# A mixture of eight experts with a residual: seven tiles of 128 pairs taken ahead of the routing tables, not eight, and the work of the routing in another order

## The chip, the cores and the metric

The kernel runs on one core of one Trainium2 chip. The metric is the device time of one execution in microseconds; before the change the median of three runs is 450.62 us (449.47 to 450.69). Engines are called as in the profile: PE is TensorE's matmul side and PEld its loading of the stationary operand, DVE is VectorE, ACT is ScalarE, POOL is GpSimd, SP is the queue that starts most transfers.

## The reference

4096 tokens (64 x 64) of 256 features, 8 experts, the best 2 per token, so 8192 (token, expert) pairs. Cut to what matters:

```python
var = jnp.mean(x * x, axis=-1, keepdims=True)
xn = rms_w * (x * jax.lax.rsqrt(var + EPS))
gate = xn @ wg_W + wg_b + (genre_embed @ gg_W + gg_b)
gate_w = jax.nn.softmax(gate, axis=-1)
topk_w, topk_i = jax.lax.top_k(gate_w, 2)
cw = sum over the two of one_hot(topk_i, 8) * topk_w
h1 = relu(einsum('bsh,ehm->bsem', x, W1) + b1)      # 256 -> 512, each expert
h2 = relu(einsum('bsem,emn->bsen', h1, W2) + b2)    # 512 -> 512
out_e = einsum('bsen,enh->bseh', h2, W3) + b3       # 512 -> 256
return x + einsum('bseh,bse->bsh', out_e, cw)
```

The reference computes all eight experts for every token; the weights `cw` of six of them are zero, and the kernel computes only the two that count. With these inputs the experts get 830, 1246, 851, 1202, 1139, 912, 767 and 1245 pairs.

## The kernel before, in words

**Two parts of the tokens.** A partition holds 32 tokens (`NI`), of which the first 8 (`NA`) are part A and the other 24 part B. Part A (1024 tokens) is routed first, in `first_part`: sums of squares (`squares`), transposes (`turn`), gate products, the two best experts (`choose`), running counts of each expert (`inc`), ranks of the tokens inside their expert (`ranks`, two small matmuls that need `inc`), and totals. From part A alone the kernel builds eight **single tiles** of 128 pairs, one for each expert (`E` = 8): every expert has at least 175 pairs in part A. Their indices are `idxA`.

**The single tiles** are the head of the program. `head_step(u, more)` runs tile u: layer 1, then the transposes of tile u+1, layer 3 of tile u-1, and layer 2 of tile u. A product here is plain: 8 products of 128 columns in layer 1 (L1046), 16 in layer 2 (L1056), 4 of 256 columns in layer 3 (L1325). The profile counts each fp32 product as two instructions.

**The routing of part B** is worked out meanwhile, mainly on DVE, by the generator `rest()`: norms and choice of part B, its ranks and totals, the layout of the remaining pairs into units, a position for each pair, and then four chunks of 16 columns of one-hot tables. A chunk is three DVE instructions: `ohl` (which row of a tile, L777), `ohh` (which tile, L779) and `ohv` (`ohh` times the token's number, L782); 16 fp16 products on PE (L616) add each chunk up to the table of indices `idxR`. `head_step` calls `more(ns)` to let the generator run for about so many ns (the numbers after `yield`), and `table(n)` to issue the table's products on PE. Then `gather_unit` fetches rows on POOL's queue with `idxR`. All engines run in the order in which the code issues.

**The units.** What the single tiles leave is laid out by expert in units of up to 4 tiles (512 pairs), in steps of 32 pairs. Units of two or more tiles run a Strassen scheme: 7 products of blocks in place of 8 (`Fast` for layers 1 and 2, L1155; `Wide` for layer 3, L1257). An expert's pairs are split into units of 16 steps (512 pairs), at most one pair of tiles (8 steps) and a last unit of 9 to 16 steps. The list of units is one of 46 arms of a switch: 32 of them are the rows of `SHAPES` (number of 16-step units, number of experts with an 8-step unit, steps of the last units), chosen on the chip by the counts. Here the first row is taken: five units of 16, then 16, 9, and then pairs of (15, 8), (14, 8), (12, 8), (11, 8), (11, 8), (10, 8). Expert 7 has 1245 - 128 = 1117 pairs left, 35 steps: 16 + 8 + 11.

**The seam.** The last head step waits for the table, gathers units E and E+1, and starts their weights' transfers on SP's queue; `fill` copies x to the output in four parts (the residual), and `give` adds each finished tile to the output by an indirect transfer on POOL's queue, in chains that wait for the unit before. Unit E (`step_fast` with u == E) transposes its four tiles on PE; the later units go through a DRAM buffer (`stow`, `shuffle`) and are transposed on DVE.

## Time and profile before

| what | us |
|---|---|
| median of the runs | 450.62 (449.47 to 450.69) |
| the profiled execution | 450.4 |
| its span, first to last instruction | 448.7 |
| PE busy | 440.1 (98%) |
| DVE busy | 358.3 (80%) |
| ACT busy | 259.2 (58%) |
| POOL busy | 274.5 (61%) |
| first single tile starts (L1046) | 23.17 |
| first unit starts (L937) | 87.03 |

The time of the profiled execution is 1.7 us above its span. The span has three stages: up to 23.17 us the gates of part A and the first gathers; to 87.03 us the eight single tiles, beside which DVE works out the routing of part B; and then 19 units. In rows of the timeline the columns are the start, the duration (for groups, from first start to last end), the engine, the line, the operation and its operands, and in brackets how long the engine sat idle before and what ended that. PE's ends are modelled, so that rows of PE overlap a little: the price of a group is the distance from its start to the start of the next.

### The profile page before, as it was taken

How to read it: one execution, taken by the hardware profiler on the slowest of the kernel's cores; microseconds unless marked ns; L12 is line 12 of the kernel's file. 1: busy time of each engine (PE TensorE's matmuls, PEld its weight loads, DVE VectorE, ACT ScalarE, POOL GpSimd, SP SyncE). 2: the span in 40 equal slices, each digit the busy share in tenths (PEclk: the TensorE clock that was granted, in tenths of full speed). 3: DMA queues.
4: the chain of work that ended last, by engine and by line, in shares of the span. 5: the costliest groups of instructions: out<-in, count | busy, mean ns of one | idle time of the engine just before them, and what ended most of it. 6: DMA issues, size and time to landing. Idle time of an engine off the chain costs nothing.

```text
span 448.7 us, 9511 instructions
## 1 busy us (share of the span) xinstructions
PE 440.1 (98%) x3096; PEld 414.2 (92%) x3096; DVE 358.3 (80%) x985; ACT 259.2 (58%) x624; POOL 274.5 (61%) x235
## 2 busy tenths in 40 slices
PE   8999999999999999999999999999999999999994
PEld 7689999988989999999999899999999999999984
DVE  5898995677798888888899977977978879779851
ACT  5855543456465555646475655755755765566642
POOL 4347433857888875837475764874775766666342
PEclk9999999999999999999999999999999999999999
DMA  8799999784657657545564663474464565555123
GB/s 291 271 345 374 383 362 384 276 260 84 185 163 138 164 94 199 93 118 103 145 117 99 117 139 92 68 166 106 66 166 107 120 135 117 124 108 105 18 24 39
DMA packets 71600, 72.51 MB, mean 162 GB/s; under 512 B 34736, under 2 KB 60819, under 8 KB 71157
## 3 DMA queue, kind: packets, MB, share of 16 engines
q1 hardware_dynamic: 48976, 43.29, 29.9%
q0 software_dynamic: 14960, 17.50, 23.6%
q10 hardware_dynamic: 7604, 11.02, 8.1%
q8 instruction: 26, 0.43, 0.4%
q14 instruction: 34, 0.27, 0.2%
HBM read 56.34 MB, written 20.12 MB: 170 GB/s over the span
## 4 chain that ended last, share of the span: by engine, by line
PE 93%; DVE 3%; issue 1%; POOLq 1%; POOL 1%; ACT 0%; DVEq 0%
PE pb L1155 55%; PE pb L1257 18%; PE pb L1056 6%; PE pb L1325 4%; PE pb L1046 3%; PE pb L254 1%; PE pb L616 1%; PE pb L482 1%; POOL out_dram L1357 1%; PE pb L937 1%; PE pb L285 1%; DVE xT L925 0%; PE pb L291 0%; DVE big L1132 0%; POOLq L1680 0%
## 5 line engine op out<-in xcount | busy, mean ns | idle before, releaser
L1357 POOL DMA_INDIRECT out_dram<-ys,idxR x57 | 98.4, 1727 | 82.0 <-DVE ys L1356 64.9
L1155 PE MATMUL pb<-hid,big 128*128 128x256 f32 (+7 forms) x456 | 83.2, 326 | 0.0
L1176 ACT ACTIVATE hid<-hid,bb 128x256 f32<-128x256 f32 (+12 forms) x154 | 72.9, 524 | 11.2 <-DVE hid L1170 10.6
L870 POOL DMA_INDIRECT cg<-cwdR,idxR x59 | 63.9, 1083 | 18.0 <-issue 18.0
L1155 PEld LDWEIGHTS pb<-hid,big 128*128 128x128 f32 x456 | 70.4, 191 | 4.2 <-ACT hid L1176 0.8
L1164 ACT COPY big<-pb 128x512 f32<-128x512 f32 (+7 forms) x57 | 27.1, 476 | 65.8 <-PE pb L1155 51.0
L1155 PE MATMUL pb<-mixB,big 128*128 128x256 f32 (+7 forms) x304 | 55.5, 325 | 0.1
L1155 PE MATMUL pb<-hotA,big 128*128 128x256 f32 (+7 forms) x304 | 55.3, 325 | 0.0
L1155 PEld LDWEIGHTS pb<-mixB,big 128*128 128x128 f32 x304 | 47.9, 191 | 3.1 <-ACT bc L1034 0.5
L1155 PEld LDWEIGHTS pb<-hotA,big 128*128 128x128 f32 x304 | 46.6, 191 | 2.1
L1155 PE MATMUL pb<-mixX,iotx 128*128 128x256 f32 (+7 forms) x228 | 46.5, 327 | 0.0
L870 POOL DMA_INDIRECT big<-in_x_dram,idxR x32 | 35.5, 1110 | 9.8 <-issue 8.2
L1155 PEld LDWEIGHTS pb<-mixX,iotx 128*128 128x128 f32 x228 | 36.6, 191 | 2.9 <-issue 0.8
L870 POOL DMA_INDIRECT xgE<-in_x_dram,idxR x27 | 30.5, 1128 | 13.0 <-issue 12.1
L1164 ACT COPY q1s<-pb 128x512 f32<-128x512 f32 (+7 forms) x57 | 26.9, 472 | 18.6 <-PE pb L1155 17.0
L1278 DVE TENSOR_TENSOR ys<-pb,big 128x128 f32<-128x128 f32 (+1 forms) x54 | 18.7, 346 | 23.4 <-PE pb L1257 16.7
L1056 PEld LDWEIGHTS pb<-hid,w2a 128*128 128x128 f32 x256 | 29.8, 192 | 1.1 <-ACT hid L1049 0.8
L1155 PE MATMUL pb<-xT,w1r 128*128 128x256 f32 (+7 forms) x152 | 30.8, 325 | 0.0
L1056 PE MATMUL pb<-hid,w2a 128*128 128x128 f32 x256 | 30.5, 276 | 0.0
L1266 ACT COPY big<-pb 128x128 f32<-128x128 f32 (+1 forms) x54 | 16.6, 307 | 23.3 <-PE pb L1257 23.3
L925 DVE STREAM_TRANSPOSE xT<-gTs 128x256 f32<-128x256 f32 x55 | 29.4, 644 | 0.6 <-DMA gTs<-scr 0.6
L1034 ACT ACTIVATE bc<-b_sb,cw 128x256 f32 x59 | 26.1, 498 | 6.4 <-DVE cw L1017 5.5
(349 smaller groups left out, 926.4 us busy)
## 6 DMA issues: line engine op xcount, KB each, us to landing
w2a<-in_L_cond_W_dram SPq DMA_DIRECT2D x8, 1024.0 KB, 12.9
w1r<-in_L_cond_W_dram SPq DMA_DIRECT2D x11, 512.0 KB, 15.0
w3r<-in_L_cond_W_dram ACTq DMA_DIRECT2D x11, 512.0 KB, 4.3
w3r<-in_L_cond_W_dram SPq DMA_DIRECT2D x10, 512.0 KB, 11.5
w1r<-in_L_cond_W_dram ACTq DMA_DIRECT2D x10, 512.0 KB, 3.6
gTs<-scr SPq DMA_DIRECT2D x7, 512.0 KB, 4.0
out_dram<-in_x_dram SPq DMA_DIRECT2D x4, 768.0 KB, 11.4
scr<-big SPq DMA_DIRECT2D x5, 512.0 KB
```

The source lines that it names most:

```text
L870: return nc.gpsimd.indirect_dma_start(out=dst, out_offset=None, in_=src, in_offset=bass.IndirectOffsetOnAxis(ap=index(b), axis=0), bounds_ ...
L925: V.transpose(xT[:, :, s0 + k, :].rearrange("p c (b k) -> p k c b", b=SQ), shs[:, s0 + k].rearrange("p k (a c) -> p k c a", a=SQ),)
L1034: nc.scalar.mul(bc, b3e, cw)
L1056: nc.tensor.matmul(ph, lhsT=w2[:, m, ts(n, P)], rhs=hid[0][:, m, 0:BT], start=(m == 0), stop=(m == MC - 1))
L1155: nc.tensor.matmul(bank[:, ts(n, self.w)], lhsT=w[:, c, ts(n, P)], rhs=x[:, c], start=new and n == 0 and c == 0, stop=n == HB - 1 and c == ...
L1164: nc.scalar.copy(self.q[(1, 6, 5).index(k)], self.tall(self.X if k == 5 else self.U))
L1176: nc.scalar.activation(out, src, AF.Relu, bias=ww[self.u][1][:, self.l, n : n + 1])
L1257: nc.tensor.matmul(bank[:, ts(j, H // 2)], lhsT=a[:, c, ts(j, P)], rhs=b[:, c], start=new and j == 0 and c == 0, stop=j == self.n - 1 and ...
L1266: nc.scalar.copy(self.q[(1, 6, 5).index(k)], self.X if k == 5 else self.U)
L1278: V.tensor_tensor(self.y(j, i), src, self.q[q].rearrange("p (k h) -> p k h", k=self.n), ALU.add)
L1325: nc.tensor.matmul(sums(u, k)[0 : cols.stop - cols.start], lhsT=hid[1][:, n, cols], rhs=w3[:, n, :], start=(i == 0), stop=(i == MC - 1),)
L1357: add = nc.gpsimd.indirect_dma_start(out=orows, out_offset=bass.IndirectOffsetOnAxis(ap=index(b)[0:n], axis=0), in_=y[0:n], in_offset=None ...
```

## The change

Eight things change together.

1. `F = 7`: single tiles are made for experts 0 to 6 only. All pairs of expert 7 go to the rest; `NREST` goes from 69 to 70 tiles and `NSURE` from 56 to 57. The table `SHAPES` is written anew; its first row is again the one that these inputs take. Expert 7 now has 1245 pairs left, 39 steps: 16 + 8 + 15. The units are five of 16, then 16, 9, (15, 8), (15, 8), (14, 8), (12, 8), (11, 8), (10, 8).
2. The tables are laid out tile by tile: `whole`, `ohh` and `ohv` are [128, tile, 16], not [128, 16, tile]. The innermost step of all operands is then one element; the copy `tokw` of the token numbers in xgE, made by ACT, is gone, and `tok2` is read with a repeated middle dimension. PE reads `ohv` with a step of 16 elements (32 bytes), as it does `ohl`. Token numbers now run from 1, so that the conversion of the table takes two DVE instructions, not four.
3. `rest()` yields at fixed places, not after so many ns. `head_step` says where each piece goes; ranks and totals of part B stand inside layer 2 of tile 1, between its third and fourth product group, and no longer ahead of layer 2 of tile 2.
4. Four of the squares go from DVE to ACT (`NA + 1` and the last three, `late`).
5. The head is reordered: one group of four transposes more stands ahead of the ranks of part A, the copy of the gates is made in two halves around the square root, and small copies move.
6. Three operations that DVE made after the ranks (`tokv`, `more`, `low`) stand ahead of them; `exps` and `weights` of part B move from behind the table to inside it.
7. On POOL's queue the gather of unit F+1 and the weights' table of part B follow the output of tile 4. On SP's queue all four fills follow the start of the weights of units F and F+1.
8. Unit F makes its transposes in two halves (`transpose_half`), with the products of layer 3 of the tile before and its own between them.

PE around the ranks of part B (`incB` is the running count that DVE works out). Before, from the end of layer 2 of tile 1:

```order
L1056 MATMUL pb_71<-hid_90,w2a 128x128 x4
L1046 MATMUL pb_68<-xT,w1r_84 128x128 x2
L1046 MATMUL pb_69<-xT,w1r_84 128x128 x2
L1046 MATMUL pb_70<-xT,w1r_84 128x128 x2
L1046 MATMUL pb_71<-xT,w1r_84 128x128 x2
L937 MATMUL pb_72<-ident,xg_206 128x128 x2
L1325 MATMUL pb_74<-w3r_87,hid_91 128x256 x4
L406 MATMUL pb_75<-incB,tri 128x8
L407 MATMUL pb_75<-incB,ntri 128x8
L412 MATMUL pb_75<-incB,ones 128x9
L1056 MATMUL pb_68<-hid_90,w2a 128x128 x4
```

And now, from layer 3 of tile 0:

```order
L1313 MATMUL pb_73<-w3r_86,hid_91 128x256 x4
L1044 MATMUL pb_68<-hid_90,w2a 128x128 x4
L1044 MATMUL pb_69<-hid_90,w2a 128x128 x4
L1044 MATMUL pb_70<-hid_90,w2a 128x128 x4
L409 MATMUL pb_75<-incB,tri 128x8
L410 MATMUL pb_75<-incB,ntri 128x8
L415 MATMUL pb_75<-incB,ones 128x9
L1044 MATMUL pb_71<-hid_90,w2a 128x128 x4
L1034 MATMUL pb_68<-xT,w1r_84 128x128 x2
```

The three small matmuls moved ahead by one layer 1, one layer 3 and a quarter of a layer 2.

DVE from the scan that makes `incB` to the first use of the totals (pb_75). Before:

```order
L400 SCALAR_TENSOR_TENSOR incB<-ohB 128x192
L401 TENSOR_TENSOR d2B<-cw8B,prB 128x24
L1356 SCALAR_TENSOR_TENSOR ys<-pb_73,cg,bc_574 128x256
L660 TENSOR_TENSOR totA<-totA_177 128x8
L661 TENSOR_SCALAR more<-totA 128x8
L662 TENSOR_TENSOR mm<-more,pb_75 128x8
```

And now:

```order
L403 SCALAR_TENSOR_TENSOR incB<-ohB 128x192
L404 TENSOR_TENSOR d2B<-cw8B,prB 128x24
L1344 SCALAR_TENSOR_TENSOR ys<-pb_73,cg,bc_569 128x256
L635 TENSOR_SCALAR tokv<-tokc 128x32
L636 TENSOR_TENSOR tokv<-tokv,tokc 128x32
L637 CAST tok_126<-tokv 128x64
L639 TENSOR_TENSOR more<-totA_176 128x8
L640 TENSOR_SCALAR more<-more 128x7
L641 TENSOR_SCALAR low<-gateA 128x56
L672 TENSOR_TENSOR mm<-more,pb_75 128x8
```

The token numbers, which stood ahead of the norms, and `low` now lie between the count and the totals.

POOL around the gathers of the first two units. Before, from the output of tile 2:

```order
L1357 DMA out_dram<-ys,idxA 4096x256
L870 DMA xg_207<-in_x_dram,idxA 128x256
L1357 DMA out_dram<-ys,idxA 4096x256
L870 DMA xgE<-in_x_dram,idxR 128x256 x4
L870 DMA big<-in_x_dram,idxR 128x256 x4
L805 COPY cw8B<-cw8A 128x64
```

And now:

```order
L1345 DMA out_dram<-ys,idxA 4096x256 x2
L858 DMA big<-in_x_dram,idxR 128x256 x4
L1345 DMA out_dram<-xg_205,idxA 4096x256
L858 DMA xgE<-in_x_dram,idxR 128x256 x4
L1445 COPY cw8B<-cw8A 128x64
```

The last single tile's gather is gone from here, and an output stands between the two units' gathers. The first unit's number is now odd, so that its rows go to the end of `big` and the second's to xgE.

The diff, cut to its core:

```diff
-    (5, 6, (15, 14, 12, 11, 11, 10, 16, 9)),
...
+    (5, 6, (15, 15, 14, 12, 11, 10, 16, 9)),
...
-    NREST = (NPAIR - TOPK * BT + E * (BT - 1)) // BT
-    NSURE = (NPAIR - E * BT) // BT
+    F = 7
+    NREST = (NPAIR - max(F - E + TOPK, 0) * BT + E * (BT - 1)) // BT
+    NSURE = (NPAIR - F * BT) // BT
...
-    whole = const.tile([P, GC, NREST], F16, name="whole")
+    whole = const.tile([P, NREST, GC], F16, name="whole")
...
-    left = [NA + i for i in (0, 1, 4, 5, 2, 3)] + list(range(NA + 8, NI))
+    left = [NA + i for i in (0, 4, 5, 2, 3)] + list(range(NA + 8, NI - 3))
+    late = list(range(NI - 3, NI))
...
+        turn_pe(GA + 3, 1, 2)
...
-        turn(GA + 3, 1, 3, "A", 2)
+        turn_copy(3, "A", 2)
...
-        some(1)
-        turn(j0, 0, 4, "A", 3)
+        squares(NA + 1, "A")
...
+        squares(late.pop(), "A")
         gates_2(((4, 5), (6, 7)), PB[7])
         nc.scalar.copy(gTs, PB[7])
+        squares(late.pop(), "A")
...
-        V.tensor_scalar(tokv, tokc, 0.0, None, ALU.is_ge)
-        V.tensor_tensor(tokv, tokv, tokc, ALU.add)
-        V.tensor_copy(tok16, tokv)
-        nc.scalar.copy(tokw, tok16.unsqueeze(2).to_broadcast([P, NI, NREST]))
         V.memset(pB.same[:, :, 0:1], 0.0)
         pB.norm(False)
-        yield 2600
         for _ in pB.choose(None):
-            yield 420
-        yield 900
-        yield None
+            pass
+        yield
+        V.tensor_scalar(tokv, tokc, float(NT // 2), float(-NT - 1), ALU.is_gt, ALU.mult)
+        V.tensor_tensor(tokv, tokv, tokc, ALU.add)
+        V.tensor_copy(tok2.rearrange("p (k i) -> p k i", k=TOPK), tokv.unsqueeze(1).to_broadcast([P, TOPK, NI]))
+        more, low = te("more"), buf(gx, [P, F, NA], "low")
+        V.tensor_tensor(more, totA1[:, 1:], totA1[:, 0:E], ALU.subtract)
+        V.tensor_scalar(more[:, 0:F], more[:, 0:F], float(-BT), 0.0, ALU.add, ALU.max)
+        V.tensor_scalar(low, pA.slot[:, 0:F], float(BT), float(-4 * NPAIR - BT), ALU.is_lt, ALU.mult)
+        yield
         pB.ranks()
         pB.totals()
-        more, mm, base, offs, nbf = (te(a) for a in ("more", "mm", "base", "offs", "nbf"))
...
-        nc.scalar.copy(whole, wide.unsqueeze(1).to_broadcast([P, GC, NREST]))
+        nc.scalar.copy(whole, wide.unsqueeze(2).to_broadcast([P, NREST, GC]))
...
-            ohh = bigf[:, 0:HW].bitcast(F16).rearrange("p (g t) -> p g t", g=GC)
+            ohh = bigf[:, 0:HW].bitcast(F16).rearrange("p (t g) -> p t g", g=GC)
             ohl = bigf[:, b0 : b0 + LW].bitcast(F16).rearrange("p (r g) -> p r g", g=GC)
-            ohv = bigf[:, b0 + LW : b0 + LW + HW].bitcast(F16).rearrange("p (g t) -> p g t", g=GC)
+            ohv = bigf[:, b0 + LW : b0 + LW + HW].bitcast(F16).rearrange("p (t g) -> p t g", g=GC)
             if c >= 3:
                 table((c - 2) * GC)
+            hi, tok = (t[:, cols].unsqueeze(1).to_broadcast([P, NREST, GC]) for t in (hi16, tok2))
             V.tensor_tensor(ohl, iotx, lo16[:, cols].unsqueeze(1).to_broadcast([P, P, GC]), ALU.is_equal)
-            yield 1250
-            V.tensor_tensor(ohh, whole, hi16[:, cols].unsqueeze(2).to_broadcast([P, GC, NREST]), ALU.is_equal)
-            yield 1200
-            i0 = c * GC % NI
-            V.tensor_tensor(ohv, ohh, tokw[:, i0 : i0 + GC], ALU.mult)
+            V.tensor_tensor(ohh, whole, hi, ALU.is_equal)
+            V.tensor_tensor(ohv, ohh, tok, ALU.mult)
             for g in range(GC):
-                mms.append((ohl[:, :, g], ohv[:, g, :], c * GC + g))
-            yield 750
-        yield None
+                mms.append((ohl[:, :, g], ohv[:, :, g], c * GC + g))
+            if c == NCH // 2 - 1:
+                yield
+                pB.exps()
+        pB.weights()
+        yield
         table()
-        V.tensor_scalar(sa, tab, 0.0, -1.0, ALU.is_gt, ALU.mult)
-        V.scalar_tensor_tensor(sa, tab, float(NT // 2), sa, ALU.add, ALU.add)
...
     def head_step(u, more):
-        if u + 3 < E:
+        if u + 3 < F:
             gather(u + 3)
-        for k in range(3 * u, min(3 * u + 3, E)):
+        for k in range(3 * u, min(3 * u + 3, F)):
             gather_cw(k)
-        table(GC * (NCH - 1) * (u == E - 2))
+        table(GC * {F - 2: 3}.get(u, 0))
         layer1(u)
         if u + RING < E:
-            load_weights(u + RING, (0,))
+            if u + RING < F:
+                load_weights(u + RING, (0,))
             if u == 0:
                 nc.sync.dma_start(b3_sb[:, 2:4], b3[2:4].unsqueeze(0).to_broadcast([P, 2, H]))
             load_weights(u + RING, (1,))
         if u == 0:
             third_part()
+            layer2(u, {0: lambda: squares(late.pop(), "A"), 1: last_upright, 2: lambda: transpose_x(1)})
+            stage_1(1)
+            more()
+            return
+        transpose_x(u + 1)
+        stage_1(u + 1)
+        if u == F - 2:
+            more()
+        scaled(u - 1, "A")
+        layer3(u - 1)
+        if u - 1 + RING < F:
+            load_weights(u - 1 + RING, (2,))
+        if u == 1:
+            nc.sync.dma_start(b3_sb[:, 4:E], b3[4:E].unsqueeze(0).to_broadcast([P, E - 4, H]))
+        give(u - 1)
+        if u == 1:
+            more()
+            layer2(u, {2: more})
         else:
-            transpose_x(u + 1)
-            stage_1(u + 1)
-            if u == E - 2:
-                while not fetched:
-                    more(1000000)
-            elif u != 2:
-                more(3200)
-            scaled(u - 1, "A")
-            layer3(u - 1)
-            if u - 1 + RING < E:
-                load_weights(u - 1 + RING, (2,))
-            if u == 1:
-                nc.sync.dma_start(b3_sb[:, 4:E], b3[4:E].unsqueeze(0).to_broadcast([P, E - 4, H]))
-        table(GC * (u == E - 3))
-        if u == 0:
-            layer2(u, {1: last_upright, 2: lambda: transpose_x(1)})
-            stage_1(1)
-            more(3200)
-        else:
-            more(3200)
+            if u < F - 2:
+                more()
             layer2(u)
-        if u == E - 2:
-            stream_3(E, mybir.EngineType.SP)
-            fill(2)
-            stream_1(E + 1, mybir.EngineType.SP)
-            stow(E + 1)
-            shuffle(E + 1)
-            fill(3)
-            give(u - 2)
-        if u >= 1 and u != E - 3:
-            give(u - 1)
-        if u == E - 3:
-            stream_1(E, mybir.EngineType.SP)
-        if u in (E - 4, E - 3):
-            fill(u - (E - 4))
+        if u == F - 2:
+            stream_1(F, mybir.EngineType.SP)
+            stream_3(F, mybir.EngineType.SP)
+            stream_1(F + 1, mybir.EngineType.SP)
+            fill(0)
+            fill(1)
...
+        if u == F - 1:
+            gather_unit(F + 1)
+            nc.gpsimd.tensor_copy(cw8B[:, 0:NA, :], pA.cw8)
+            pB.spread(cwdR, cw8B, 0)
+            layer1(u)
+            stow(F + 1)
+            shuffle(F + 1)
+            fill(2)
+            fill(3)
+            stage_1(F)
+            for l in (0, 1):
+                for _ in Fast(F, l).fold():
+                    pass
+            scaled(u - 1, "A")
+            layer3(u - 1)
+            stream_1(F + 2, mybir.EngineType.SP)
+            stream_3(F + 1, mybir.EngineType.SP)
+            give(u - 1)
+            gather_cw(F)
+            V.tensor_tensor(four, both[:, 0 : P // 4], both[:, P // 4 : P // 2], ALU.add)
+            return
...
+        f, g = Fast(u, 0), Fast(u, 1)
+        if u == F:
+            transpose_half(u, 0)
+            layer3(u - 1, part=(0,))
+            f.p(1)
+            transpose_half(u, 1)
...
+    def transpose_half(u, j):
+        n = size(u) // 2
+        for c in range(HC):
+            bank = (PB[4], PB[7])[c][:, j * n * BT : (j + 1) * n * BT].rearrange("p (s t) -> p s t", t=BT)
+            for k in range(n):
+                g = xgR[u % 2][:, j * n + k].rearrange("p (r c) -> p c r", c=HC)
+                nc.tensor.transpose(bank[:, k], g[:, c], ident)
+            (nc.scalar.copy if c else V.tensor_copy)(xT[:, c, j * n : (j + 1) * n], bank)
```

More of the change, by code (lines that the diff above doesn't have):

```diff
@@ L1365, in give @@
             )
-            if b < E:
+            if b < F:
                 for f in fills[1:]:
-                    tc.declare_no_dep(add.ins, f.ins, reason="the first E tiles hold tokens of the first part alone")
+                    tc.declare_no_dep(add.ins, f.ins, reason="the first F tiles hold tokens of the first part alone")
             behind = list(adds[-2]) if len(adds) > 1 else [fills[0]]
-            if b >= E and not behind_fills:
+            if b >= F and not behind_fills:
                 behind += fills[1:]
@@ L1448, in fill @@
         for a in sum(adds, []):
-            tc.declare_no_dep(f.ins, a.ins, reason="the first E tiles hold tokens of the first part alone")
+            tc.declare_no_dep(f.ins, a.ins, reason="the first F tiles hold tokens of the first part alone")
         fills.append(f)
     def fetches_of(u, last):
-        far = E + 1 < u + 2 < last
+        far = F + 1 < u + 2 < last
         if far:
```

189 lines of the change are left out of this document (73 added, 116 removed), and 60 rows, old and new, of the table SHAPES.

## The prediction, written before the changed kernel ran

> **What bounds the kernel now.** I read the page first, then PE's waits, then the stages, then the timelines of the head.
>
> ```profile
> span 448.7 us, 9511 instructions
> PE 440.1 (98%) x3096; PEld 414.2 (92%) x3096; DVE 358.3 (80%) x985; ACT 259.2 (58%) x624; POOL 274.5 (61%) x235
> PE pb L482 <- DVE ones L158: 1.1, 1, 1.1
> PE pb L406 <- DVE d2A L401: 0.8, 1, 0.8
> PE pb L551 <- DVE hotA L547: 0.2, 1, 0.2
> ```
>
> PE is idle for 448.7 - 440.1 = 8.6 us, and its waits of any length are three, 2.1 us in all, each in the first 18 us. Between the head and the end PE is a full pipe: an edit counts by the PE time that it removes or adds, and work of other engines counts only where it makes PE wait.
>
> ```profile
> 46.44:53.76 7.32, 7.32 (x60) 7.11 (x60) 6.87 (x42) 3.60 (x10) 3.50 (x6) 1.00 1.07 369
> 87.03:104.66 17.63, 17.63 (x87) 15.24 (x86) 12.15 (x26) 9.25 (x18) 11.18 (x13) 1.00 0.69 201
> 282.56:317.21 34.65, 34.65 (x255) 34.65 (x254) 28.37 (x77) 21.12 (x53) 22.30 (x17) 1.00 0.53 110
> 348.22:378.10 29.88, 29.88 (x234) 29.48 (x233) 24.65 (x72) 18.98 (x52) 19.47 (x16) 1.00 0.56 124
> ```
>
> These are stages, cut at the starts of PE's groups (length, then busy time of PE, PEld, DVE, ACT, POOL). The first is one single tile with its turn of DVE: 7.32 us, PE without a gap. The second is the start of unit E, also without a gap, so that its reordering into halves has nothing to gain: I cost it at nothing, covered by the products themselves. The last two are the periods of a (14, 8) and an (11, 8).
>
> **One single tile less, one unit wider.** The tile that goes is worth 7.33: layer 1, transposes, layer 3, layer 2, the 7.32 of the row. It returns in the units: expert 7 has 39 steps of 32 left, not 35, so its last unit is 15 wide and not 11. No other unit differs. A 15 behind an 8 does not stand in the trace; it is a 14 and the widening of its 84 fp32 instructions (42 products of layers 1 and 2) from 224 columns to 240:
>
> ```profile
> 258.10 1.79 PE L1155 MATMUL pb<-hotA,big 128*128 128x240 f32 x8
> 259.72 0.61 PE L1257 MATMUL pb<-w3r,mixB 128*128 128x128 f32 x4
> ...
> 293.39 1.68 PE L1155 MATMUL pb<-hotA,big 128*128 128x224 f32 x8
> 294.90 0.61 PE L1257 MATMUL pb<-w3r,mixB 128*128 128x128 f32 x4
> ```
>
> From start to start 8 of 240 take 1.62 and 8 of 224 take 1.51, so 84 x 0.11 / 8 = 1.16. A (15, 8) costs 34.65 + 1.16 = 35.81, against 29.88: **+5.93**. Layer 3 is in it: a unit of four tiles runs the scheme on all four, one of three on two only and the third plainly. Tile against widening: **-1.40**.
>
> **The ranks of part B, earlier.** PE now meets them between the third and the fourth group of layer 2 of tile 1. There it needs the count of part B from DVE.
>
> ```profile
> 30.42 0.42 DVE L245 CUSTOM_DVE_ANT_0 sqV<-big 128x256 f16<-128x256 f32 x1
> 30.89 0.43 DVE L245 CUSTOM_DVE_ANT_0 sqV<-big 128x256 f16<-128x256 f32 x1
> 31.24 0.18 DVE L621 TENSOR_SCALAR tokv<-tokc 128x32 f32<-128x32 f32 x1
> 31.82 0.18 DVE L346 TENSOR_SCALAR varB<-ss 128x24 f32<-128x24 f32 x1
> 35.30 0.56 DVE L380 TENSOR_TENSOR_SCAN prB<-fresh,gateB 128x192 f32<-128x192 f32 x1
> 39.24 0.94 DVE L400 TENSOR_TENSOR_SCAN incB<-ohB 128x192 f32<-128x192 f32 x1
> 39.89 0.64 POOL L388 TENSOR_TENSOR wB<-gateB,prB 128x192 f32<-128x192 f32 x1
> 42.80 0.16 DVE L662 TENSOR_TENSOR mm<-more,pb 128x8 f32<-128x8 f32 x1 [1.54 <-PE pb L412]
> ```
>
> In this stretch DVE waits for nobody until the totals (1.54 us, last row). Four squares at 0.47 (30.42 to 30.89) leave it, 1.88, and the three token instructions, 0.58 (31.24 to 31.82): the norms start at 31.82 - 2.46 = 29.36. ACT takes the four squares beside PE's products; none is needed later than 29. From the norms to the end of the count it is 40.18 - 31.82 = 8.36, so the count is ready at about 37.7.
>
> ```profile
> 14.81 0.39 PE L406 MATMUL pb<-incA,tri 128*128 128x8 f32 x2 [0.81 <-DVE d2A L401]
> 18.59 0.63 PE L254 MATMUL pb<-ident,big 128*128 128x128 f32 x4
> 34.71 3.73 PE L1056 MATMUL pb<-hid,w2a 128*128 128x128 f32 x32
> 38.28 1.95 PE L1046 MATMUL pb<-xT,w1r 128*128 128x128 f32 x16
> 42.03 0.28 PE L406 MATMUL pb<-incB,tri 128*128 128x8 f32 x2
> 42.62 3.82 PE L1056 MATMUL pb<-hid,w2a 128*128 128x128 f32 x32
> ```
>
> And PE? A group of four transposes (18.59, 0.63 with a modelled end, some 0.5 in the pipe) moves into its 0.81 us of idle time ahead of the ranks of part A, so layer 2 of tile 1 starts at about 34.2, not 34.71, and its third quarter ends at 34.2 + 0.75 x 3.57 = 36.9. It then waits some 0.85 us for the count: the half microsecond won at 15 us is lost here, since the end of the wait is DVE's. Ranks (42.03 to 42.62, 0.59) and the last quarter (0.89) end at 37.75 + 0.59 + 0.89 = 39.2, where before, with the 0.59 of ranks that came later, it is 38.28 + 0.59 = 38.87. **+0.4**; behind the wait stand the rest of layer 2 and all tiles. Bounds: -0.5, if DVE is early enough for PE to keep the half microsecond; +0.9, if it is half a microsecond later. What can shift it is POOL's subtraction (wB), which ran from 39.89 beside the scan L400: 0.94 us for 192 elements, where the scan L380 takes 0.56. It now falls two instructions earlier in the same chain, so I leave its price of 0.38 where it is. [...]
>
> **The tables.** The totals reach DVE at 38.4, not 42.8, so the routing of part B starts 4.4 us earlier, while the tiles that must hide it are one fewer.
>
> ```profile
> 57.72 1.22 DVE L777 TENSOR_TENSOR big<-iotx,lo 128x2048 f16<-128x2048 f16 x1
> 58.85 1.30 DVE L779 TENSOR_TENSOR big<-whole,hi 128x1104 f16<-128x1104 f16 x1
> 60.19 0.73 DVE L782 TENSOR_TENSOR big<-big,xgE 128x1104 f16<-128x1104 f16 x1
> 60.84 0.48 DVE L1356 SCALAR_TENSOR_TENSOR ys<-pb,cg,bc 128x256 f32<-128x256 f32 x1
> 74.77 0.23 DVE L788 TENSOR_SCALAR sa<-pb 128x69 f32<-128x69 f32 x1 [4.09 <-PE pb L616]
> ```
>
> A chunk takes 60.84 - 57.72 = 3.12, from start to start 1.13 for 2048 elements of `ohl`, 1.34 for 1104 of `ohh`, 0.65 for `ohv`. `ohh` gets the layout that `ohl` has, so I price its 1120 elements by `ohl`'s row: 1120 x 1.13 / 2048 = 0.62, and `ohv` stays at 0.66. A chunk becomes 2.4. With the outputs of tiles 1 to 3, and one wait of 0.45 for layer 3 of tile 1, the chunks end at about 56.1, 58.5, 61.4 and 63.8 us on DVE. PE, 7.3 us a tile from 39.2 on, wants the first at 57.8, the next two at 62.4, the last at 66.4. All are in time, the third by 1 us; before, DVE stood idle for 4.09 at the end of the table. So chunks cost PE nothing; if `ohh` stays at 1.34, the third is 2.1 us later and PE waits about 1.
>
> On PE the 64 products of the table read `ohv` with a step of 32 bytes.
>
> ```profile
> 65.06 0.98 PE pb L616 x16
> L616 PEld LDWEIGHTS <-big 128*128 128x128 f16 x64 | 4.4, 168 | 0.1
> ```
>
> The first row is from the chain of waits: sixteen take 0.98, 61 ns each. No moving operand here has such a step; the nearest row is the load of the same products, whose 128 columns of `ohl` have it already and fit into those 61 ns. Then 70 columns fit too, and I take 0. The upper bound is a price per column that is twice the load's: 70 x 0.96 = 67 ns more a product, 64 x 0.067 = 4.3 us.
>
> **The seam.** The last chunk's products end at about 67.3, the indices follow at 67.9, and unit F would start at 87.03 + 0.4 - 7.33 = 80.1.
>
> ```profile
> 76.44 1.06 POOL L870 DMA_INDIRECT xgE<-in_x_dram,idxR x1 [5.07 <-issue]
> ...
> 80.47 1.48 POOL L870 DMA_INDIRECT xgE<-in_x_dram,idxR x1 [0.30 <-issue]
> ...
> 87.03 1.12 PE L937 MATMUL pb<-ident,xgE 128*128 128x128 f32 x8
> ```
>
> Before, the last of E's four gathers was issued 6.6 us ahead of the transposes. Now the four start at about 68.6 and the last at 72.7, 7.4 ahead, and the first half needs two only. Two fills now start beside them on SP's queue. The gathers of F+1 wait on POOL for tile 4's output and come a little later against the unit's start than before; `stow`, `shuffle` and the weights' gathers follow them. I take 0; bound +2.
>
> **Sum** against the profiled execution's own span: 448.7 - 7.33 + 5.93 + 0.4 = **447.7**. That execution took 450.4, 1.7 above its span and 0.2 below the median; so 447.7 + 1.7 + 0.2 = **449.6 us**, 0.23% below 450.62. About 0.3% (1.35 us) is what a measurement of this kernel can tell from no change, so the likeliest reading is no difference.
>
> **Rivals.**
> 1. *No new wait at the ranks.* If the count is ready at 36.9, PE keeps the half microsecond and the price is -0.5: 448.7. For it: POOL's wB may fall beside no DVE instruction of the chain; against: 0.85 us must come from a chain of 8.36 in which no instruction changes. 18%.
> 2. *The step of 32 bytes slows the table's products: slower.* Place: the 64 products, behind which stand tile 5, tile 6 and every unit. At the upper bound 449.6 + 4.3 = 453.9. From 1.0 us, 16 ns a product, it makes the kernel slower than 450.62, and from 2.4 us, 37 ns, by more than 0.3%. Against it: the load with that step. For it stands only that no row has it on the moving side. [...] 9%.
> 3. *The compare isn't faster*, the repeated dimension costs as the innermost did: the third chunk makes PE wait about 1 us, 450.6. Against: `ohl` has this layout at half the price per element. 7%.
> 4. *The seam is late*: rows of F, `shuffle` of F+1 behind the fills, or the weights' table hold PE for 1 to 2 us: 450.6 to 451.6. For: POOL's queue is fuller between 74 and 96; against: the 7.4 above. 11%.
>
> The forecast itself has 55%.
>
> **The numbers.** Its own range is 448.9 to 450.3. The whole goes from 447.8, below rival 1 with the spread of the runs (449.47 to 450.69), to 452.4, inside rival 2. Faster by over 0.3% means below 449.27: rival 1 and a good third of the forecast, 0.37. Slower means above 451.97: most of rival 2 and a part of 4, 0.14. Between, 0.49.
>
> **What would show it.** In the changed profile: seven periods of 7.3 us from 23 on and a first unit at about 80; a wait of 0.5 to 1 of PE for `incB` near 37; `ohh` at 0.7 on DVE; table products still 61 ns apart; DVE waiting for PE, not PE for DVE, ahead of the conversion; a period of 35.8 for the second (15, 8). Wrong it would be if PE shows a wait ahead of the table's products or at the first unit's transposes, or if another list of units runs.

## The result, and the profile after

The changed kernel takes **454.65 us** (median of 6 runs, 453.31 to 455.01), the kernel before 449.67 in 6 runs beside it: a ratio of 1.0092, interval 1.0078 to 1.0106. It is slower by 5.0 us, 0.9%. The profiled execution took 454.59, with a span of 452.9 against 448.7.

The page of the changed kernel and PE's waits:

```profile
span 452.9 us, 9411 instructions
PE 444.8 (98%) x3058; PEld 417.6 (92%) x3058; DVE 357.3 (79%) x977; ACT 258.0 (57%) x625; POOL 271.9 (60%) x235
PE pb L486 <- DVE ones L159: 1.1, 1, 1.1
PE pb L920 <- DMA xg<-in_x_dram,idxA: 0.2, 1, 0.2
PE pb L409 <- DVE d2A L404: 0.2, 1, 0.2
PE pb L558 <- DVE hotA L554: 0.2, 1, 0.2
```

PE issues 38 instructions fewer, waits less than before, and yet is busy for 4.7 us longer: the loss is in the duration of instructions, not in a wait. The three stretches show where. "Pairs" is an experiment below, the changed kernel with the table in another layout.

| stretch, us | before | changed | pairs | forecast of the difference |
|---|---|---|---|---|
| to the first single tile | 23.17 | 22.44 | 22.35 | -0.5 |
| single tiles, to unit F (E before) | 63.86 | 62.67 | 56.79 | -7.33 + 0.9 |
| units, to the end | 361.67 | 367.79 | 367.46 | +5.93 |
| span | 448.7 | 452.9 | 446.6 | -1.0 |

The single tiles were to become 6.4 us shorter and became 1.2 shorter. In the chain of waits of the changed kernel (start, length, what):

```profile
57.30 2.16 PE pb L625 x16
59.46 3.57 PE pb L1044 x32
63.03 4.32 PE pb L625 x32
67.35 2.97 PE pb L1034 x16
70.32 0.43 PE pb L920 x2
70.75 2.13 PE pb L625 x16
```

Sixteen products of the table (L625) take 2.16, **135 ns each**, where they took 0.98, 61 ns. Behind the thirty-two, layer 1 of tile 5 (L1034) takes 2.97, and not the 1.79 of the other tiles. The stretches around it, with the granted clock in the third column from the end:

```profile
62.87:67.17 4.30, 4.30 (x35) 4.30 (x33) 1.58 (x5) 0.37 (x1) 0.22 (x1) 1.00 1.10 354
67.17:70.11 2.94, 2.94 (x18) 2.94 (x17) 0.00 (x0) 1.10 (x3) 1.34 (x1) 0.59 1.08 377
70.11:70.54 0.43, 0.43 (x4) 0.38 (x3) 0.00 (x0) 0.12 (x1) 0.00 (x0) 0.50 0.98 310
```

While the products run, the clock is full, so it isn't the clock that slows them; right behind them it falls to 0.59 and 0.50. In the kernel before the clock is 1.00 through the whole table:

```profile
64.89:74.56 9.67, 9.67 (x115) 9.67 (x114) 5.71 (x6) 3.52 (x11) 2.12 (x1) 1.00 1.07 379
```

On DVE the layout did what it was to do (`ohh` in the first row, `ohv` in the second), and at the end of the table DVE waits for PE for 8.29 us, where it was 4.09:

```profile
54.14 0.73 DVE L776 TENSOR_TENSOR big<-whole,hi 128x1120 f16<-128x1120 f16 x1
54.91 0.74 DVE L777 TENSOR_TENSOR big<-big,tok 128x1120 f16<-128x1120 f16 x1
72.92 0.23 DVE L786 TENSOR_SCALAR sa<-pb 128x70 f32<-128x70 f32 x1 [8.29 <-PE pb L625]
```

Eight of the runs below (marked "other chip") were made on chips on which the kernel before takes 473 to 474 us and not 450. Their times are given, but PE has other waits there at the first units (up to 8.5 us at once, where the longest in the pairs is 1.1), so that prices are read from durations inside them only.

### The profile page after: what moved, and what is told of

The parts are those of the page before. It is cut to its first block, busy times and chain, and to the rows that moved or that the text cites. A ratio compares the mean times of both kernels' runs of the same rounds, so it can differ in the third digit from the quotient of the medians.

```text
span 452.9 us, 9411 instructions
## 1 busy us (share of the span) xinstructions
PE 444.8 (98%) x3058; PEld 417.6 (92%) x3058; DVE 357.3 (79%) x977; ACT 258.0 (57%) x625; POOL 271.9 (60%) x235
## 4 chain that ended last, share of the span: by engine, by line
PE 92%; DVE 3%; issue 2%; POOL 1%; DMA 1%; POOLq 0%; DVEq 0%
PE pb L1143 55%; PE pb L1245 18%; PE pb L1044 6%; PE pb L1313 3%; PE pb L1034 3%; PE pb L625 2%; POOL out_dram L1345 1%; PE pb L486 1%; PE pb L255 1%; DMA xg<-in_x_dram,idxA 1%; PE pb L286 1%; PE pb L920 0%; DVE xT L912 0%; DVE big L1120 0%; PE pb L292 0%
## 5 line engine op out<-in xcount | busy, mean ns | idle before, releaser
L1143 PE MATMUL pb<-hid,big 128*128 128x256 f32 (+7 forms) x456 | 84.5, 329 | 0.0
L858 POOL DMA_INDIRECT cg<-cwdR,idxR x60 | 65.4, 1090 | 19.3 <-issue 17.0
L858 POOL DMA_INDIRECT xgE<-in_x_dram,idxR x33 | 36.9, 1118 | 10.1 <-issue 8.8
L1143 PEld LDWEIGHTS pb<-mixX,iotx 128*128 128x128 f32 x228 | 36.7, 191 | 3.1 <-issue 0.8
L1266 DVE TENSOR_TENSOR ys<-pb,big 128x256 f32<-128x256 f32 (+1 forms) x54 | 19.2, 356 | 25.3 <-PE pb L1245 19.1
L858 POOL DMA_INDIRECT big<-in_x_dram,idxR x27 | 30.4, 1127 | 13.7 <-issue 13.0
L1164 ACT ACTIVATE hid<-pb,bb 128x256 f32<-128x256 f32 (+7 forms) x76 | 27.7, 416 | 2.4 <-PE pb L1143 1.8
L1254 ACT COPY big<-pb 128x256 f32<-128x256 f32 (+1 forms) x54 | 17.0, 314 | 20.1 <-PE pb L1245 20.0
L1044 PEld LDWEIGHTS pb<-hid,w2a 128*128 128x128 f32 x224 | 26.2, 192 | 1.0 <-ACT sqA L244 0.8
```

Source lines behind the costliest of these rows:

```text
L858: return nc.gpsimd.indirect_dma_start(out=dst, out_offset=None, in_=src, in_offset=bass.IndirectOffsetOnAxis(ap=index(b), axis=0), bounds_ ...
L1044: nc.tensor.matmul(ph, lhsT=w2[:, m, ts(n, P)], rhs=hid[0][:, m, 0:BT], start=(m == 0), stop=(m == MC - 1))
L1143: nc.tensor.matmul(bank[:, ts(n, self.w)], lhsT=w[:, c, ts(n, P)], rhs=x[:, c], start=new and n == 0 and c == 0, stop=n == HB - 1 and c == ...
L1164: nc.scalar.activation(out, src, AF.Relu, bias=ww[self.u][1][:, self.l, n : n + 1])
L1254: nc.scalar.copy(self.q[(1, 6, 5).index(k)], self.X if k == 5 else self.U)
L1266: V.tensor_tensor(self.y(j, i), src, self.q[q].rearrange("p (k h) -> p k h", k=self.n), ALU.add)
```

## The experiments

Theory T1: PE reads `ohv` as its moving operand (the other one, `ohl`, is what PEld loads for these products), and the step of 32 bytes there is what costs 74 ns a product; the clock falls because of it. Rivals: T2, something else in the table's surroundings; T3, the clock falls for a reason of its own. Besides, the other terms of the sum are to be priced one by one.

### The values product by product again

```diff
-    ohv = bigf[:, b0 + LW : b0 + LW + HW].bitcast(F16).rearrange("p (t g) -> p t g", g=GC)
+    ohv = bigf[:, b0 + LW : b0 + LW + HW].bitcast(F16).rearrange("p (g t) -> p g t", g=GC)
-    V.tensor_tensor(ohv, ohh, tok, ALU.mult)
+    V.tensor_tensor(ohv.rearrange("p g t -> p t g"), ohh, tok, ALU.mult)
-    mms.append((ohl[:, :, g], ohv[:, :, g], c * GC + g))
+    mms.append((ohl[:, :, g], ohv[:, g, :], c * GC + g))
```

> The changed kernel with one thing put back: the table's values lie product by product again, so that each product on PE reads them without a step; the compares stay tile by tile, and VectorE writes the values with a step (a write of 0.66 us may become up to 1.3). T1, the 32-byte step on the side that PE streams in doubles a product, and the lower clock behind it follows from it: a product at 61 ns, so 64 x 74 ns = 4.7 us back, clock 1.00 in the layer 1 that comes behind and 1.4 us back: span 452.9 - 6.1 = 446.8. T2, the products are slow for another reason (VectorE's fp16 writes beside them, the place in the program): they stay at 135 ns and the span at 452 to 453. T3, the products are slow by the step, but the clock falls there whatever they do: 4.7 back, the dip stays, 448.2.

Measured: 464.93 us, span 463.0, 1.0335 times the kernel before (1.030 to 1.037). None of the three spans came. DVE's write, which I had bounded at 1.3 us, takes five. DVE, then stretches of PE:

```profile
54.88 5.08 DVE L777 TENSOR_TENSOR big<-big,tok 128x1120 f16<-128x1120 f16 x1
```

```profile
57.00:60.02 3.02, 0.08 (x2) 0.00 (x1) 3.02 (x2) 0.00 (x0) 2.75 (x1) 1.00 1.08 392
60.02:60.98 0.96, 0.96 (x16) 0.96 (x16) 0.96 (x2) 0.00 (x0) 0.93 (x1) 0.60 1.01 382
```

PE stands for 3 us until the first chunk is there. But the sixteen products that follow, which read without a step, take 0.96 us, 60 ns each, even at a clock of 0.60. T2 has nothing left on PE's side; as a comparison of times the run fails, since it put a new cost in place of the old.

### The step of the kernel before

```diff
-    ohv = bigf[:, b0 + LW : b0 + LW + HW].bitcast(F16).rearrange("p (g t) -> p g t", g=GC)
+    ohv = bigf[:, b0 + LW : b0 + LW + HW].bitcast(F16).rearrange("p (t g) -> p t g", g=GC)
-    V.tensor_tensor(ohv, ohh, tokw[:, i0 : i0 + GC], ALU.mult)
+    V.tensor_tensor(ohv.rearrange("p t g -> p g t"), ohh, tokw[:, i0 : i0 + GC], ALU.mult)
-    mms.append((ohl[:, :, g], ohv[:, g, :], c * GC + g))
+    mms.append((ohl[:, :, g], ohv[:, :, g], c * GC + g))
```

> The kernel before with one thing of the change alone: its table values written tile by tile, so that each product reads them with a 32-byte step (VectorE's write of them gets the step too: up to 0.7 us a chunk more, under the 4.09 us that it idles before the last product). T1: the 64 products go from 61 to 135 ns, +4.7 us, and the clock falls behind them as in the changed kernel, +1.4: 449.7 + 4.7 to 6.1 = 454.4 to 455.8. T2: 449.7 to 450.5. T3, a lower clock that does not come from the products: +4.7 without a dip, 454.4.

Measured: 465.61 us, 1.0345 (1.0325 to 1.0365). DVE's write has a step here too (32 bytes) and takes 4.91 us for 1104 values, not 0.73, so the time is again not that of the products. PE's wait for DVE's write, the first sixteen products and the layer 2 behind them:

```profile
64.17:64.58 0.41, 0.00 (x1) 0.00 (x1) 0.41 (x2) 0.00 (x0) 0.41 (x1) 1.00 1.09 287
64.58:66.67 2.09, 2.09 (x17) 2.09 (x16) 2.09 (x3) 0.00 (x0) 0.39 (x1) 1.00 1.07 403
66.67:72.05 5.38, 5.38 (x34) 5.25 (x33) 5.35 (x3) 1.11 (x3) 4.36 (x1) 0.68 1.06 392
```

131 ns each: in the kernel before, too, the step alone doubles them. The clock falls behind them as well, to a mean of 0.68, and the layer 2 takes 5.38, not the 3.57 that it takes at full clock. Here sixteen slow products were enough, with 0.41 us of standing ahead of them.

### Pairs: a step of 4 bytes

```diff
-    whole = const.tile([P, NREST, GC], F16, name="whole")
+    whole = const.tile([P, NREST, 2], F16, name="whole")
-    ohv = bigf[:, b0 + LW : b0 + LW + HW].bitcast(F16).rearrange("p (t g) -> p t g", g=GC)
+    ohv = bigf[:, b0 + LW : b0 + LW + HW].bitcast(F16).rearrange("p (h t w) -> p h t w", h=GC // 2, w=2)
...
-    mms.append((ohl[:, :, g], ohv[:, :, g], c * GC + g))
+    mms.append((ohl[:, :, g], ohv[:, g // 2, :, g % 2], c * GC + g))
```

(`ohh` likewise, and the token numbers and `whole` read with repeated dimensions.)

> The changed kernel with the table's compare and values laid out in pairs of products: a product reads its 70 values with a step of 4 bytes instead of 32, and VectorE still finds both of a pair side by side. T1 with a threshold in the step: a product at 61 ns, VectorE's compare and values at 0.7 to 0.8 us each as in the changed kernel, span 446 to 447. T1 with a price for any step over 2 bytes: 64 to 135 ns a product, span 447 to 453. By T2 nothing changes: 135 ns, 452 to 453. VectorE could lose its gain: the compare back at 1.3 us, without a cost in time as long as the chunks are ready before PE comes.

Measured: **448.93 us**, 0.9979 times the kernel before (0.9968 to 0.9990). Page, chain and DVE:

```profile
span 446.6 us, 9411 instructions
PE 438.5 (98%) x3058; PEld 411.8 (92%) x3058; DVE 356.6 (80%) x977; ACT 257.3 (58%) x625; POOL 270.7 (61%) x235
```

```profile
57.16 0.97 PE pb L625 x16
58.12 3.65 PE pb L1047 x32
61.77 1.98 PE pb L625 x32
63.76 1.86 PE pb L1037 x16
65.62 0.23 PE pb L923 x2
65.85 0.98 PE pb L625 x16
```

```profile
53.93 0.73 DVE L779 TENSOR_TENSOR big<-whole,hi 128x1120 f16<-128x1120 f16 x1
54.69 0.74 DVE L780 TENSOR_TENSOR big<-big,tok 128x1120 f16<-128x1120 f16 x1
```

A product is back at 61 ns, layer 1 behind it takes 1.86 at full clock, and DVE keeps its gain to the hundredth. The single tiles are 5.88 us shorter than in the changed kernel: 8.61 - 3.93 = 4.68 in the 64 products, 2.97 + 0.43 - 1.86 - 0.23 = 1.31 behind them, and -0.1 in other groups. T1 holds with a threshold in the step, T2 falls, and this version is faster than the changed kernel and, by 0.2%, than the kernel before. (The profiled execution is the shortest of its ten: their spans go from 446.6 to 448.5, median 447.15.) The load of `ohl` has its 32-byte step in this run as well: on the stationary side no cost of it shows within the 61 ns. No run lays `ohl` out without the step, so a smaller cost on that side stays possible.

### Eights and fours: steps of 16 and 8 bytes

The same layout with `w=8` and with `w=4`.

> The same layout in groups of eight: a step of 16 bytes. If it is the step in bytes that costs in proportion, a product takes about half of the extra 74 ns, near 98 ns, and the span is near 449. [...] If the threshold lies over 16 bytes, 61 ns and 446 to 447. [...]

Measured: 454.1 us, 1.0083 (1.0057 to 1.0109), span 453.1. The thirty-two and the layer 1 behind them in the chain:

```profile
63.10 4.22 PE pb L625 x32
67.33 2.99 PE pb L1037 x16
```

132 ns a product with 16 bytes, against 135 with 32. The clock falls as well, to 0.68 from 67.15 to 68.60 and 0.50 to 70.11.

> The table laid out in groups of four products: a step of 8 bytes, between the 4 bytes that cost nothing and the 16 that cost all. If two elements in 16 bytes are enough, a product takes 61 ns and the span is 446.6, as with pairs. If the price comes with any step over 4 bytes, a product takes 135 ns, and the clock dip follows: 452.9. A price between would give 95 to 100 ns and some 449. [...]

Measured (other chip): 476.02 us, 1.0079 (1.0036 to 1.0122). In the chain:

```profile
58.47 1.11 PE pb L625 x16
59.59 3.62 PE pb L1047 x32
63.21 2.24 PE pb L625 x32
65.44 1.83 PE pb L1037 x16
```

70 ns a product. Layer 1 behind the thirty-two takes 1.83, where the pairs have 1.86 at a clock of 1.00 and the eights 2.99: no fall shows. So with steps of 2, 4, 8, 16 and 32 bytes a product takes 61, 61, 70, 132 and 135 ns: the cliff lies between 8 and 16.

### The clock: sixteen slow products at a time

```diff
     if u < F - 2:
         more()
-    layer2(u)
+    layer2(u, {2: lambda: table(2 * GC)} if u == F - 3 else {})
```

> The changed kernel, 32-byte step and all, with its second sixteen of the table's products moved between the third and the fourth group of layer 2 of tile 4, so that no more than sixteen slow products (2.2 us) stand in a row anywhere, where the changed kernel has thirty-two (4.3 us). T1 with a clock that falls when PE has worked at half its pace for some 3 to 4 us: products still 135 ns, clock 1.00 in layer 1 of tile 5, which takes 1.8 and not 2.95: span 452.9 - 1.4 = 451.5. If the clock falls for another cause at that place, or by the sum of slow products, the dip stays and so does the span, 452.9.

Measured (other chip): 479.8 us, 1.0193 (1.0113 to 1.0272); products at 135 ns, the layer 1 behind them 1.79 us in the chain. Once more on a chip like that of the first runs:

> The changed kernel with the 32-byte step, its second sixteen of slow products moved into layer 2 of tile 4, so that no thirty-two stand in a row. On a chip with late weights layer 1 of tile 5 took 1.8 us and not 2.95. If the run of slow work is what lowers the clock, unit F starts 1.4 us earlier than in the changed kernel, 83.7 and not 85.1, and the span is 451.5, ratio to the kernel before 1.006. If it was that chip, the dip is back and the span is 452.9, ratio 1.009.

Measured: 453.74 us, 1.0078 (1.0061 to 1.0095). The chain and the stretches of the third sixteen and of layer 1:

```profile
66.88 2.15 PE pb L625 x16
69.04 1.79 PE pb L1034 x16
```

```profile
66.72:68.86 2.14, 2.14 (x19) 2.14 (x18) 0.00 (x0) 0.37 (x1) 1.57 (x1) 1.00 1.05 388
68.86:70.66 1.80, 1.80 (x18) 1.80 (x17) 0.00 (x0) 0.92 (x3) 0.00 (x0) 1.00 1.07 368
```

All 64 products are as slow as ever, and the clock stays at 1.00 behind them. From the first single tile to unit F it is 61.46 us, not 62.67: 1.2 back of the 1.4 expected. (The profiled span of 453.2 does not show it: there the first tile came 1.5 us later than in the changed kernel, at 23.98. Eight products of the gates took 1.86 there, from 20.32, not 0.99 as in the kernel before; that looks like a lower clock, but the clock of that stretch isn't shown. The other three executions have 451.9 to 452.1.) T3 falls for this place: two traces with thirty-two slow products in a row, the changed kernel's and that of the eights, have the fall right behind them (layer 1 takes 2.97 and 2.99 us); two with sixteen at a time, and the two with fast products, pairs and fours, have none (1.79 and 1.79, 1.86 and 1.83; the clock, read in the second of the sixteens and in the pairs, is 1.00).

A law of thirty-two it is not. In "The step of the kernel before" sixteen were enough, behind a short wait. And the fall isn't in every execution. The six of the changed kernel have spans of 451.6 and 452.1 us at a mean granted clock of 0.996 and 0.999, and of 452.9 to 453.2 at 0.992 or 0.993. The fall in the profiled execution (0.41 of the clock for 2.94 us, 0.50 for 0.43) takes 0.003 off a mean over 452.9 us, so the one at 0.999 ran without it, and the one at 0.996 probably too; they are as short as the three of the sixteen apart. Whether the other three long ones had it at this place or, as perhaps here, in the head, their means don't tell. What decides whether it comes stays open.

### The tile alone

```diff
-    F = 7
+    F = 8
...
-            if u < F - 2:
+            if u < F - 2 and u != F - 3:
                 more()
```

(with the list of units of the kernel before, on top of the pairs; the second edit keeps the pieces of the routing at the tiles where seven tiles have them)

> The pairs with eight single tiles instead of seven and the list of units of the kernel before; all other parts of the change stay. It prices the tile alone. By the prediction's two terms a tile costs 7.33 and gives back 5.93 in the last unit, so that the span is 1.4 us longer than that of the pairs, 446.6 + 1.4 = 448.0, and the ratio to the kernel before about 1.001 instead of 0.998. If seven tiles win nothing here, since the routing has one tile less to hide behind or the first unit starts worse, 446.6 or less.

Measured: 450.41 us, 1.0005 (0.9994 to 1.0016), against 0.9979 for the pairs; span 448.4. From the first tile to unit F:

```profile
22.60:86.78 64.18, 64.14 (x543) 61.50 (x544) 47.62 (x177) 30.60 (x89) 34.72 (x32) 1.00 1.00 354
```

The tile costs 64.18 - 56.79 = 7.39 (forecast 7.33), and the units take 448.4 - 86.78 = 361.6 against 367.46, a difference of 5.84 (forecast 5.93). Seven tiles gain 7.39 - 5.84 = 1.55 us, and the medians are 1.48 apart (by the ratios 1.2: the two ran on two chips). Two runs of the same edit on other chips could not tell:

> The changed kernel with pairs of products (446.6), and eight single tiles instead of seven, with the list of units of the kernel before; all other parts of the change stay. It prices the tile alone. By the prediction's two terms a tile costs 7.33 and gives back 5.93 in the last unit, so the span becomes 446.6 + 1.4 = 448.0. If the seven tiles win nothing here, since the routing has a tile less to hide behind or the first unit starts worse, it stays at 446.6 or falls below.

> The pairs with eight single tiles instead of seven and the list of units of the kernel before; all other parts of the change stay. It prices the tile alone. By the prediction's two terms a tile costs 7.33 and gives back 5.93 in the last unit, so that the span is 1.4 us longer than that of the pairs. If seven tiles win nothing here, since the routing has one tile less to hide behind or the first unit starts worse, it is no longer, or shorter.

Measured (other chips): 472.91 us, 0.999 (0.9938 to 1.0042), and 473.8 us, 1.0004 (0.9967 to 1.0041), where the pairs beside the second had

> The changed kernel with the table in pairs of products once more, on the same chip as the next three, as their base. Span 446.6 and a product at 61 ns again, unit F from 79.1 us, if the chip lets the weights come in time; ratio to the kernel before near 0.998.

475.61 us, 1.0057 (0.9995 to 1.0119). On such a chip the pairs' gain over the kernel before isn't there, and none of the three can be told from it. What PE waits for there the records don't say in full (its longest waits at the first units bear the name "issue" or end with a fold on DVE). The "late weights" of some expectations are a guess that these runs don't show; I leave it open.

### The ranks where they were

```diff
-    layer2(u, {2: more})
+    layer2(u)
...
+    if u == 2:
+        more()
     if u < F - 2:
         more()
     layer2(u)
```

> The changed kernel with pairs of products (446.6), with the ranks and totals of part B put back ahead of layer 2 of tile 2, as before; seven tiles stay. My prediction gave the move a price of 0.4 through a wait for the count, so that putting it back would gain 0.4: 446.2. The changed trace shows no such wait; then the move by itself costs PE nothing, and what it does is to start the routing some 4 us earlier. Without it VectorE's chunks of the table would be ready 4 us later, the first at 59.5 and not 55.4, while PE comes at 57.0 and, for the next two, at 61.6: waits of 2 to 4 us, and a span of 449 to 451.

> The pairs with the ranks and totals of part B ahead of layer 2 of tile 2, as before; seven tiles stay. By the prediction's term of 0.4 this would gain 0.4: 446.2. On a chip with late weights PE stood 3.3 us ahead of the product that spreads the tile numbers and ran at a low clock behind it (5.4 us for a layer 2 of 3.6). If that is the routing and not the weights, it comes here as well: +3.3 +1.6, unit F at 84 and not 79.1, span 451 to 451.5.

Measured (e9_ranks_late, other chip): one execution, of 481.41 us, with a wait of 3.3 us. On the chip of the second: 456.0 us, 1.0148 (1.0111 to 1.0185), span 453.7. PE's and DVE's waits, and the stretch behind:

```profile
PE pb L752 <- DVE ebt L746: 4.8, 1, 4.8
```

```profile
DVE ys L1347 <- ACT bc L1025: 3.4, 1, 3.4
DVE prB L725 <- POOL twos L671: 1.3, 1, 1.3
```

```profile
54.72:60.22 5.50, 5.50 (x34) 5.50 (x34) 5.33 (x12) 1.38 (x4) 1.62 (x1) 0.64 1.06 397
```

With seven tiles and the ranks in the old place, PE stands 4.8 us ahead of the product that spreads the tiles' numbers (`place`), and the layer 2 behind it takes 5.50 at a clock of 0.64, not 3.6: the single tiles take 63.72, 6.9 more than with the ranks early. DVE, which has the count at 36.7 as with the ranks early, stands idle for 3.4 us (the first row) and then, a step later, waits for a copy on POOL that stands behind an output (1.83 us in the chain of waits). So the move of the ranks is no trifle of 0.4: the seventh tile's gain hangs on it.

### The head's order, and the first unit's

```diff
-    turn_pe(0, 0, 0)
+    turn(0, 0, 0, "V", 0)
+    turn(0, 1, 1, "A", 1)
     nc.tensor.transpose(rwp, rw2, ident[:HC, :HC])
...
-    nc.scalar.copy(gTs[:, 0 : 2 * P], PB[3][:, 0 : 2 * P])
-    pA.norm(True, lambda: nc.scalar.copy(gTs[:, 2 * P :], PB[3][:, 2 * P :]))
+    nc.scalar.copy(gTs, PB[3])
+    pA.norm(True)
```

> The pairs with the head's order of the kernel before: the first copies, the bias copy and the copy of the gates in one piece ahead of the square root. The prediction gave the head's order no price of its own; the changed trace has the gates' products at 7.80 and not 8.35, and the first tile 0.73 us earlier. If that is the order's doing, the first tile comes some 0.5 to 0.7 later and the span is longer by as much, 447.2. If it comes from the squares, which stay on ScalarE here, nothing changes.

> The pairs with the head's order of the kernel before: the first copies, the bias copy, and the copy of the gates in one piece ahead of the square root. The changed trace has the gates' products at 7.80 where the kernel before has 8.35, and the first tile 0.73 us earlier. If that is the order's doing, the first tile comes 0.5 to 0.7 later than the 22.35 of the pairs and the span is 447.2. On a chip with late weights the order showed nothing at the first tile (22.68 against 22.69 us); if that holds, 446.6.

Measured: on the other chip 476.04 us, 1.0107 (1.0053 to 1.0161), with the first tile at 22.68 us, against 22.69 for the pairs beside it. On the chip of the second 449.42 us, 0.9984 (0.9970 to 0.9997), span 447.4. The first tile in PE's timeline there:

```profile
23.00 0.38 PE L1035 MATMUL pb<-xT,w1r 128*128 128x128 f32 x1
```

The gates start at 8.16, where three kernels with the new order on the same chip have 7.15 to 7.33, and the first tile at 23.00, where they have 22.39 to 22.60. That looks like 0.4 to 0.6 us for the order, but it isn't shown. With the old order the first tile came at 23.17 in the kernel before and at 22.28 in "The step of the kernel before"; with the new one it came at 22.22 to 22.83 in twelve traces and at 23.41 to 23.98 in three. It differs by more from execution to execution than the order could bring, and by the times the order isn't told from the pairs either.

```diff
     transpose_half(u, 0)
-    layer3(u - 1, part=(0,))
-    f.p(1)
     transpose_half(u, 1)
...
+    layer3(u - 1, part=(0, 1))
+    f.p(1)
+    for k in (1, 2, 3, 4):
+        f.mix(k)
```

> The pairs with the start of unit F in the order of the kernel before: all its transposes ahead of its products. Prediction: the order costs nothing either way, so the span stays. The changed trace has 17.85 us for this stretch where the kernel before has 17.63: if that is the price of the halves, the span is 0.2 shorter and the stretch back at 17.6. If the halves hide late rows or a late copy, PE waits at the transposes and the span is longer by that wait.

> The pairs with the start of unit F in the order of the kernel before: all its transposes ahead of its products. Prediction: the order costs nothing either way. If the halves are what makes 17.85 of 17.63 us in the changed kernel, the stretch is back at 17.6 and the span 0.2 shorter; if the halves hide late rows or a late copy, PE waits at the transposes, 1.4 us as it did on a chip with late weights, and the span is 448.

Measured: on the other chip 479.58 us, 1.0124 (1.0011 to 1.0236), with a wait of 1.4 us of PE at the transposes. On the chip of the second 449.71 us, 0.9994 (0.9983 to 1.0005), span 447.7. The start of unit F there, and in the pairs:

```profile
79.23:97.40 18.17, 17.89 (x86) 15.32 (x85) 12.85 (x27) 9.40 (x19) 13.95 (x16) 1.00 0.83 259
```

```profile
79.14:96.87 17.73, 17.73 (x87) 15.06 (x85) 11.87 (x27) 9.31 (x19) 13.84 (x15) 1.00 0.79 245
```

With all transposes first PE waits 0.28 us for the copies, and the stretch is 0.44 longer. The halves are no loss: 17.73 against the 17.63 of the kernel before, in which the copies were made in whole banks, a form that I did not run.

## Why the prediction was wrong

The forecast was 449.6, the result is 454.65. **The step that failed** is the price of the table's products: "Then 70 columns fit too, and I take 0." The nearest row I had was the load of the same products, and I carried its price over to the other operand. The two sides don't share it: the loads, with a step of 32 bytes, fit into 61 ns a product, and the moving side pays 74 ns a product for the same step. 64 x 74 ns = 4.7 us. My own upper bound, a price per column that is twice the load's, was 67 ns, and the truth lies above it; between the two ends I went to "the nearest row", which is a row of the other operand. Rival 2 came in, above its own upper end of 453.9; 9% were far too little, and the range ended inside it.

The prediction also says that no moving operand of the kernel before has such a step. That is not so: the ranks' products read `incA` with a step of 32 bytes and `incB` with one of 96. But with 8 columns a product, at the 1.05 ns a column measured here for fp16, the price would be 8 ns, an estimate, too little for their rows to show.

**What rival 2 lacked** is the clock: in the profiled execution it fell behind thirty-two slow products for 3.4 us, and 1.3 us were lost in layer 1 of tile 5 and the transposes behind it. The kernel before has a granted clock of 1.00 in all stretches of this stage, and I asked nowhere what PE at half its pace would do to it. On the span: 447.7 forecast + 4.7 + 1.3 = 453.7; the 452.9 measured are 0.8 less, about the wait for the count that did not come (below).

**The rest of the sum** came out to within 1.1 us, which the pairs show: span 446.6, median 447.15, against a forecast of 447.7. One of its terms, the ranks, was wrong, and one, the head's, these runs can't tell from nothing.

- One tile less, one unit wider: -1.40 forecast, -1.5 measured by the tile alone. The period of the second (15, 8), forecast as 35.81:

```profile
280.93:316.70 35.77, 35.77 (x254) 34.72 (x253) 28.83 (x74) 21.63 (x53) 23.71 (x19) 1.00 0.54 116
```

- The ranks: the wait of 0.85 for the count did not come. DVE, POOL and PE in the changed kernel:

```profile
28.61 0.18 DVE L347 TENSOR_SCALAR varB<-ss 128x24 f32<-128x24 f32 x1
33.06 0.85 DVE L395 TENSOR_TENSOR ohB<-gTs 128x192 f32<-128x192 f32 x1
33.46 0.64 POOL L391 TENSOR_TENSOR wB<-gateB,prB 128x192 f32<-128x192 f32 x1
36.24 0.56 DVE L403 TENSOR_TENSOR_SCAN incB<-ohB 128x192 f32<-128x192 f32 x1
36.86 0.39 PE L409 MATMUL pb<-incB,tri 128*128 128x8 f32 x2
```

PE came at 36.86, as forecast (36.9); the count was ready at 36.80, not at 37.7. Most of that comes from the start of DVE's chain: the norms began at 28.61 (first row), 0.75 earlier than I had worked out. I had moved PE by the head's half microsecond and left DVE where it was, but DVE moves with the head. By the rows of the kernel before the norms stand 31.82 - 2.46 - 23.17 = 6.19 behind the first tile; they stand 6.17 behind it in the changed kernel, 6.15 with the pairs, and 6.23 in the sixteen apart, where the first tile came 1.5 us later. The other 0.16 come from POOL's subtraction. It fell five instructions earlier in the chain, not two, beside `ohB`, which takes 0.85 and not 0.63: a price of 0.22, where beside the scan it was 0.38. So what rival 1 says, no wait, came in, with 18%; but the reason given for it, a subtraction beside no instruction of DVE's, did not. What I did not see is how much stands behind the move: 7 us, if the ranks stay late while a tile goes.
- The chunks: 2.57 from start to start (53.00 to 55.57) and not 2.4; in time, and the third rival with them gone. The seam: no wait at unit F's transposes; rival 4 did not come.
- The head: -0.8 measured with the pairs, -0.5 forecast. That these are close may be luck: the first tile's start differs by more than that between executions of the same head, and that the order brings anything isn't shown.

## What to carry to other kernels

A layout has two readers. When one is changed so that a vector engine reads along its innermost dimension, look at what step it leaves to PE's moving operand, and price that by a row of a moving operand, never by one of the load. The two wishes can often be met at once: groups of two kept DVE's speed and PE's. And where PE will run slowly for some microseconds, or stand, count what the clock does behind it (in these runs 0.59 behind 4.3 us of slow products, 1.00 behind 2.2), and break the stretch up.
